# Two steps of the gated pairs' experts with each state in the first five parts of the recurrence, not only in the first

## The chip, the cores and the metric

The kernel runs on one core of one Trainium2 chip. The core has five engines that matter here: TensorE (PE for its matmuls, PEld for its weight loads), VectorE (DVE), ScalarE (ACT), GpSimd (POOL) and SyncE (SP, which only issues transfers in this kernel). Each engine works through its own queue of instructions in order, and they wait for each other by semaphores. The metric is the device time of one execution in microseconds (us), as the median of several runs.

## The reference

The program is a network of four layers on a batch of four sequences, 1024 rows of 128 features each, all in 32-bit floating point. Every layer has a mixing part and a feed-forward part, each followed by a residual and a layer norm. What matters here are the feed-forward part of the third layer and both parts of the fourth.

The third layer's feed-forward part picks two of eight experts for every row, and each expert is a gated pair of products ("gated pairs' experts" below):

```
h13 = einsum('bsh,ehi->bsei', x, w13);  gate, up = split(h13, 2)
h   = silu(gate) * up                              # 256 wide
y   = einsum('bsei,eih->bseh', h, w2)
out = sum over the two chosen experts of weight * y
```

The fourth layer's mixing part is a state-space recurrence, with 256 channels and 16 states per channel:

```
h   = exp(d_l[:, :, None] * A) * h + (d_l * x_l)[:, :, None] * b_l[:, None, :]
y_l = einsum('ben,bn->be', h, c_l)
```

The fourth layer's feed-forward part computes eight experts of width 512 for every row, without a choice in the products ("dense experts" below), and weighs them with a gate that keeps the most probable ones up to a sum of 0.8.

## The kernel before

The activations stay on the chip: `xN[b]` holds a batch's rows, `xT[b]` the same transposed. Layers one and two come first. Then the third layer's mixing part (`l2_attn`) runs over 128 units, and work of later parts is interleaved with it. The interleaving is done with Python generators: each part of the network is a generator that issues some instructions and yields, and a driver decides how often each one is advanced. The order in which instructions are issued in this way is their priority. A planner in the framework (`schedule_with_timeline_sim=True`) then sets the final order on each engine, taking by that priority what its own model of time finds ready. In `l2_attn` TensorE's order is taken from the program as it is; in the part that changes here the planner orders all engines. So the code's order is a strong guide to the queues, but not exactly the queues.

**The gated pairs' experts** are the generator `moe`, made by `l2_ffn`. For each batch, a router (`l2_dispatch`) ranks the experts of every row, and sixteen indirect transfers from POOL's queue (L1366, tile `xrows`) scatter the rows to a place in memory where rows of one expert are together. This gives 23 tiles of 128 rows per batch, 92 units for four batches. One step of the generator, at position `t`, does the following: every fourth step it loads four tiles of scattered rows for unit t+8 (SP); it loads the weights of unit t+4 (SP, L1441, tile `wx`, four buffers of 384 KB); it transposes rows for unit t+2 (every fourth step); it computes the hidden part of unit t (TensorE, then a tanh on ACT at L1473 and two products on DVE at L1474 and L1477); and it computes the output of unit t-2 (TensorE, a copy on ACT at L1493, and every fourth step a store from SP at L1495). A weight buffer is free for its next load once the output products have read it. When a batch's last tile is done, `l2_combine` starts and is advanced twice with each step: sixteen indirect gathers from POOL's queue (L1512, tile `yg`), a scaling on ACT, two additions on DVE (L1535, L1536) and a layer norm, after which the batch is marked "done". The generator yields without work while the scatters of the batch that it needs next are not all issued.

**The recurrence** works in halves: two for each of four batches, 512 positions each, eight in all (`l3`). `l3_prepare` computes a half's inputs. `l3_scan` runs its sixteen states. A state loads two rows `bn` and `cn`, broadcast to all partitions (SP, L1818, four buffers each); multiplies on POOL (L1823, tile `db`); computes a decay on ACT (L1827) and a scan on DVE (L1828) for each of two channel halves; and multiplies again on POOL (L1839, tile `hc`, four buffers). TensorE sums `hc` over the states in PSUM (tile `pys`); for batches 1 to 3 two states are first added by an accumulating transfer from POOL's queue (L1843). `l3_sum` and `l3_finish` end a half, with its output product, layer norm and router; the half then waits in the list `todo`.

**The dense experts** are the generator `work`, made by `l3_experts`. It takes halves from `todo` once they have aged by more than three states. A half's eight experts take six steps each: four with one hidden block (tile `ph`, ACT at L1951, tile `hh`) and two around the output products (tile `py`, added on DVE at L1967). Their weights are the tile `wh`, three buffers of 512 KB, loaded by SP (L1651).

**The driver** is the loop in `l3`. Before the scan of the second half of a batch it drains `moe` until the next batch is done. Then, with every state of the scan, it advances the end of the previous half, the preparation of the next half, the rest of the fourth batch's dispatch (which issues one scatter per state), `moe` once (and once more where i is 0), and `work` three times while `moe` still has steps and four times afterwards. All PSUM tiles of these parts but the scan's own share four banks (`ff`), and the experts, the preparation and the end of a half take them in turn.

Of the kernel before, what the change touches and what calls it, by code (L numbers as in the profile page):

```python
# [58 lines left out]
class Net:  # L59
# [1513 lines left out]
    def l3(self, moe, fp):  # L1573

        c3 = self.c3
        halves = [dict(b=b, h=h) for b in range(B) for h in range(2)]
        for i, u in enumerate(halves):  # L1580
            u["prev"] = halves[i - 1] if u["h"] else None
        halves[0] = dict(self.c3["first"], **{k: halves[0][k] for k in ("prev",)})
        for i, u in enumerate(halves[1:], 1):
            u["prev"] = halves[i - 1] if u["h"] else None
        work = self.l3_experts(fp)
        end = iter(())
        for i, u in enumerate(halves):
            nxt = iter(())
            if i + 1 < len(halves):
                if halves[i + 1]["h"] == 0:  # L1590
                    while "done" not in self.m2["st"][halves[i + 1]["b"]]:
                        next(moe)
                nxt = self.l3_prepare(halves[i + 1])
            for f in self.l3_scan(u):
                next(end, None)
                next(nxt, None)
                for k in range(1):
                    next(self.m2["rest"], None)
                busy = next(moe, moe) is not moe
                if i == 0:  # L1600
                    for k in range(1):
                        next(moe, None)
                for k in range(3 if busy else 4):
                    next(work)
                for v in c3["todo"]:
                    v["age"] += 1
            for f in chain(end, nxt):
                pass
            end = chain(self.l3_sum(u), self.l3_finish(u))
        for f in end:  # L1610
            next(work)
        c3["all"] = True
        for f in work:
            pass
# [563 lines left out]
```

## Time and profile before

| | |
|---|---|
| median of three runs | 2389.36 us (2387.49 to 2404.25) |
| the profiled execution | 2414.07 us, of which its span is 2412.3 us |
| granted TensorE clock, mean | 0.917 |
| busy PE, PEld | 2068.1 us (86%), 1454.9 us (60%) |
| busy DVE, ACT, POOL | 1420.2 us (59%), 1287.5 us (53%), 863.0 us (36%) |
| instructions | 34775 |
| transfers | 209.84 MB, mean 87 GB/s |

The profile is one execution on the chip. Times in its views are from the start of the span. A busy TensorE is not one at its peak, since its matmuls are pipelined and their ends are modelled. The profile's line for the granted clock gives tenths of full speed. Many instructions carry the line of a small helper (L127 for all matmuls, L131 for transposes), so they are told apart by the names of the tiles that they write and read. A matmul of 32-bit operands appears as two records. In a list of waits, the columns are the waiting engine and its tile and line, what ended the wait, the total in us, the number of waits and the longest.

### The profile page before, as it was taken

What the parts mean: (1) busy time and instruction counts of PE and PEld (TensorE: products, weight loads), DVE (VectorE), ACT (ScalarE), POOL (GpSimd) and SP (SyncE); (2) the same over time, 40 slices, a digit from 0 to 9 for tenths busy, and PEclk for the clock granted to TensorE, in tenths of its full rate; (3) what the DMA queues carried; (4) which work ended last, traced back from release to release, by engine and by line L of the source; (5) the groups of instructions that cost most, each with busy time, mean ns of one, the idle gap of its engine ahead of it and who ended that gap; (6) DMA issues with size and microseconds to landing.
All of it is one profiled execution on the core that took longest, in us unless ns stands there. A gap on an engine that the chain in (4) does not pass through costs nothing.

```text
span 2412.3 us, 34775 instructions
## 1 busy us (share of the span) xinstructions
PE 2068.1 (86%) x12170; PEld 1454.9 (60%) x12170; DVE 1420.2 (59%) x3949; ACT 1287.5 (53%) x2679; POOL 863.0 (36%) x557
## 2 busy tenths in 40 slices
PE   6767979979899999999979965778797989899888
PEld 3455655544577787787767753346564656565566
DVE  6457733433455655655555676777777777687421
ACT  6543433332455555555556555565757766767443
POOL 5001220000000011001020148888877879589400
PEclk9657989989999999999999987789998989999899
DMA  3000110022000010021222155456764657476411
GB/s 101 0 18 20 32 31 9 9 86 71 1 1 1 1 34 21 11 81 43 65 64 82 35 181 176 140 176 178 193 198 135 181 154 207 139 205 176 114 57 49
DMA packets 138512, 209.84 MB, mean 87 GB/s; under 512 B 18597, under 2 KB 75936, under 8 KB 138080
## 3 DMA queue, kind: packets, MB, share of 16 engines
q1 hardware_dynamic: 126048, 172.82, 23.2%
q0 software_dynamic: 12288, 34.79, 6.9%
q8 instruction: 96, 1.57, 0.3%
q14 instruction: 80, 0.66, 0.1%
HBM read 159.24 MB, written 23.16 MB: 76 GB/s over the span
## 4 chain that ended last, share of the span: by engine, by line
PE 60%; DVE 18%; ACT 10%; issue 7%; DMA 2%; POOL 1%; another core or an unknown queue 1%; SPq 0%; ACTq 0%; POOLq 0%; DVEq 0%
PE ph L127 12%; PE py L127 8%; PE po L1118 4%; PE pqk L127 4%; PE po L127 4%; PE pt L131 4%; PE pa_m L127 3%; DVE db L1828 3%; PE pys L127 3%; PE po L1134 3%; PE kp_mo L127 3%; PE pv L127 2%; PE pr L127 2%; DVE a L1105 1%; PE kp_mo L131 1%
## 5 line engine op out<-in xcount | busy, mean ns | idle before, releaser
L1839 POOL TENSOR_TENSOR hc<-db,cn 128x1024 f32<-128x1024 f32 x128 | 317.1, 2528 | 88.8 <-PE pys L127 41.8
L1823 POOL TENSOR_TENSOR db<-ud,bn 128x1024 f32<-128x1024 f32 x112 | 287.1, 2638 | 29.3 <-DVE pmv L159 23.2
L127 PEld LDWEIGHTS py<-wh,hh 128*128 128x128 f32 x2048 | 253.7, 197 | 70.5 <-issue 40.9
L127 PE MATMUL ph<-xT,wh 128*128 128x512 f32 x512 | 265.3, 637 | 33.5 <-DVE h_acc L1967 13.4
L127 PE MATMUL py<-wh,hh 128*128 128x128 f32 x2048 | 259.8, 281 | 14.6 <-ACT hh L1951 9.5
L1951 ACT ACTIVATE hh<-ph,sb_cols 128x512 f32<-128x512 f32 x256 | 171.8, 682 | 158.6 <-PE ph L127 127.2
L1151 DVE SCALAR_TENSOR_TENSOR num<-po,sb_c_trig,nsin 128x130 f32<-128x130 f32 x256 | 89.2, 348 | 268.5 <-ACT nsin L1150 251.2
L1827 ACT ACTIVATE da<-dl,aneg 128x512 f32<-128x512 f32 x224 | 153.3, 689 | 66.7 <-DVE db L1828 63.2
L127 PE MATMUL pys<-hc,sb_c_ident 128*128 128x512 f32 x320 | 168.6, 655 | 15.6 <-POOL hc L1839 8.2
L1026 POOL MEMSET cv<- 128x16 f32 x32 | 4.1, 128 | 482.6 <-ACT cv L1043 365.5
L1828 DVE TENSOR_TENSOR_SCAN db<-da,carry,db 128x512 f32<-128x512 f32 x128 | 157.4, 1268 | 20.4 <-POOL db L1823 10.2
L127 PEld LDWEIGHTS ph<-xT,wh 128*128 128x128 f32 x512 | 93.9, 204 | 123.6 <-issue 56.5
L1150 ACT ACTIVATE nsin<-po,sb_c_trig 128x130 f32<-128x130 f32 x256 | 94.8, 370 | 131.7 <-PE po L1134 72.3
L1828 DVE TENSOR_TENSOR_SCAN db<-da,db 128x512 f32<-128x512 f32 x128 | 149.6, 1206 | 14.3 <-ACT da L1827 6.7
L127 PE MATMUL pqk<-xT,wE 128*128 128x256 f32 x512 | 138.9, 395 | 16.7 <-DVE cv L1036 13.7
L1967 DVE SCALAR_TENSOR_TENSOR h_acc<-py,gt,h_acc 128x128 f32<-128x128 f32 x256 | 72.1, 343 | 130.3 <-PE py L127 125.0
L1366 POOL DMA_INDIRECT xrows<-xN,di x64 | 62.4, 976 | 238.1 <-ACT kN L1070 230.6
L1118 PE MATMUL po<-cv,a 128*128 128x130 f32 x1024 | 138.7, 279 | 1.0 <-DVE num L1151 0.8
L1118 PEld LDWEIGHTS po<-cv,a 128*128 128x128 f32 x1024 | 126.8, 194 | 5.1 <-PE pqk L127 1.1
L1043 ACT ACTIVATE cv<-cv,sb_c_trig 128x520 f32<-128x520 f32 x128 | 86.5, 724 | 77.3 <-DVE cv L1036 68.2
L127 PEld LDWEIGHTS pys<-hc,sb_c_ident 128*128 128x128 f32 x320 | 63.3, 211 | 85.3 <-issue 60.4
L127 PEld LDWEIGHTS pqk<-xT,wE 128*128 128x128 f32 x512 | 88.5, 192 | 36.3 <-DVE cv L1036 18.1
(456 smaller groups left out, 4492.9 us busy)
## 6 DMA issues: line engine op xcount, KB each, us to landing
wx<-in_wF SPq DMA_DIRECT2D x92, 384.0 KB
bn<-rows SPq DMA_DIRECT2D x128, 256.0 KB
cn<-rows SPq DMA_DIRECT2D x128, 256.0 KB
wh<-in_wH SPq DMA_DIRECT2D x64, 512.0 KB
hc<-hc POOLq DMA_DIRECT2D x48, 512.0 KB
xrows<-zero SPq DMA_DIRECT2D x4, 1472.0 KB
xg<-xrows SPq DMA_DIRECT2D x20, 256.0 KB
yrows<-ys SPq DMA_DIRECT2D x20, 256.0 KB
```

The costliest lines, as they stand in the source:

```text
L127: return self.nc.tensor.matmul(out=out, lhsT=lhsT, rhs=rhs, start=start, stop=stop)
L131: self.nc.tensor.transpose(out, in_, self.ident[0:n, 0:n])
L1043: nc.scalar.activation(Q["v"][c][:, hs, i, :], v1[:, hs, :], AF.Copy, scale=c2["trig"][:, k, i : i + 1],)
L1118: self.nc.tensor.matmul(out=u["po"][:, i, c, :], lhsT=u["a"][:, i, c, :], rhs=Q["v"][c][:, 2 * hp + i, :, :].rearrange("p a d -> p (a d)") ...
L1134: self.nc.tensor.matmul(out=u["po"][:, i, c, :], lhsT=u["q"][h, s], rhs=Q["st"][h, hp, c, :], start=False, stop=True, skip_group_check=True,)
L1150: nc.scalar.activation(t, po[:, :, c, VW : 2 * VW], AF.Copy, scale=trig[:, k, 1:2])
L1151: nc.vector.scalar_tensor_tensor(num[:, c], po[:, :, c, 0:VW], trig[:, k, 0:1], t, ALU.mult, ALU.add)
L1823: nc.gpsimd.tensor_mul(db, ud, bc[0])
L1827: nc.scalar.activation(da, dl[:, ec, :], AF.Exp, scale=aneg[:, j : j + 1])
L1828: nc.vector.tensor_tensor_scan(db[:, ec, :], da, db[:, ec, :], carry[:, ec, n : n + 1] if h else 0.0, ALU.mult, ALU.add,)
L1839: nc.gpsimd.tensor_mul(hc, db, bc[1])
L1951: nc.scalar.activation(ht, ph, AF.Relu, bias=self.col("h_b1", i=e * NK + k))
```

## The change

One condition in the driver's loop: the second step of the gated pairs' experts with each state is taken in halves 0 to 4 and no longer in half 0 alone.

```diff
                 busy = next(moe, moe) is not moe
-                if i == 0:
-                    for k in range(1):
-                        next(moe, None)
+
+                if i < 5:
+                    next(moe, None)
                 for k in range(3 if busy else 4):
                     next(work)
```

Here `i` counts the eight halves from 0. Where `moe` has no steps left, the added call returns at once and does nothing. What the steps issue is the same in both kernels, and so are the buffers and their numbers.

## The prediction

> **What bounds the kernel now.** I began with the page's forty slices. TensorE is dense except in slices 23 to 28 (one slice is 60.3 us), which is where GpSimd begins to work:
>
> ```profile
> PE   6767979979899999999979965778797989899888
> ...
> POOL 5001220000000011001020148888877879589400
> PEclk9657989989999999999999987789998989999899
> ```
>
> That stretch is the recurrence (`l3_scan`), eight halves of sixteen states. I cut it at the end of each half's last `hc` product (L1839) and asked for the busy time between the cuts; halves 0 to 7, columns PE, PEld, DVE, ACT, POOL, then granted clock, DMA share, GB/s:
>
> ```profile
> 1411.60:1551.90 140.30, 80.66 (x320) 51.63 (x320) 102.22 (x173) 72.37 (x162) 111.29 (x67) 0.77 0.55 176
> 1551.90:1654.50 102.60, 81.29 (x337) 52.89 (x338) 72.57 (x134) 63.16 (x128) 87.34 (x49) 0.84 0.53 157
> 1654.50:1763.20 108.70, 90.78 (x454) 61.65 (x453) 88.79 (x147) 70.34 (x147) 82.95 (x41) 0.94 0.70 198
> 1763.20:1881.90 118.70, 103.69 (x497) 67.68 (x496) 81.43 (x158) 79.71 (x147) 97.15 (x57) 0.93 0.58 164
> 1881.90:1978.70 96.80, 83.35 (x372) 50.71 (x371) 75.79 (x138) 69.18 (x129) 81.38 (x42) 0.93 0.64 172
> 1978.70:2058.20 79.50, 76.54 (x386) 50.81 (x386) 60.84 (x106) 51.23 (x86) 75.80 (x39) 1.00 0.67 182
> 2058.20:2171.10 112.90, 102.13 (x493) 65.71 (x491) 81.29 (x158) 81.10 (x139) 82.16 (x42) 0.95 0.65 180
> 2171.10:2258.20 87.10, 79.52 (x396) 52.65 (x396) 64.19 (x114) 56.09 (x87) 80.32 (x41) 0.96 0.64 173
> ```
>
> From half 1 on, a half lasts as long as its busiest engine plus 3 to 18 us: half 1 is POOL + 15.3, half 2 PE + 17.9, half 3 PE + 15.0, half 4 PE + 13.4. After half 7 about 154 us of experts remain on PE. The gated pairs' experts' share of PE, in halves 0 to 3 (tile `wx`, PE then PEld):
>
> ```profile
> 1411.60:1551.90 140.30, 36.05 (x216) 32.80 (x216) 0.77 0.55 176
> 1551.90:1654.50 102.60, 25.73 (x168) 24.10 (x168) 0.84 0.53 157
> 1654.50:1763.20 108.70, 19.05 (x132) 17.53 (x132) 0.94 0.70 198
> 1763.20:1881.90 118.70, 5.79 (x44) 5.62 (x44) 0.93 0.58 164
> ```
>
> A unit (one tile of 128 rows) has 12 records, so these halves run 18, 14, 11 and 3.7 units. Its other work, from the groups of halves 1 and 2 by shape (busy us, mean ns):
>
> ```profile
> L1477 DVE SCALAR_TENSOR_TENSOR mh<-sg,ph 128x256 f32<-128x256 f32 x25 | 10.3, 414 | 1.2
> L1474 DVE SCALAR_TENSOR_TENSOR sg<-sg,ph 128x256 f32<-128x256 f32 x25 | 10.3, 412 | 14.6 <-ACT sg L1473 14.5
> ...
> L1473 ACT ACTIVATE sg<-ph 128x256 f32<-128x256 f32 x25 | 9.4, 375 | 14.9 <-PE ph L127 8.6 <-remote 6.2
> ```
>
> In the lists of waits, half 2 and then half 3 show what happens when PE is loaded, and half 0 what two units per state met:
>
> ```profile
> POOL hc L1839 <- PE pys L127: 18.1, 2, 10.9
> ```
> ```profile
> POOL hc L1839 <- PE pys L127: 22.0, 3, 10.9
> ```
> ```profile
> PE ph L127 <- DMA wx<-in_wF: 7.5, 5, 3.2
> ```
>
> The recurrence's products stand still because the sums that free their buffers (`pys`) lie behind expert matmuls in PE's queue.
>
> **What moves, counted through the generators.** No instruction is added or removed. Half 0 keeps its two steps per state. In the code's order half 1 now takes units 61 to 91 (before: 61 to 76), so half 2 loses its fifteen; batch 2's combination ends at half 1, state 10 instead of half 2, state 5; batch 3's at half 2, state 10 instead of half 4, state 5. From then on the generator is empty, and the dense experts (`wh`) get four steps per state for three. This brings them forward by about 1.3 experts at the end of half 2, and no further: the second half's experts end at half 3, state 8 (before 13), then idle until the third half's router at state 13. From half 5 on the order is the old one, so halves 5 to 7 and the tail are costed at nothing. Nobody needs the early results: batch 2's are wanted before half 3 and batch 3's before half 5, and both were done in time.
>
> **Half 1.** +14 units in the cut: PE 14 x 1.84 (25.73/14) = 25.8, and a transpose each, 0.21 (5.4 us in 26 records), 2.9: 81.3 becomes 110.0. DVE +14 x 0.826 = 84.2. ACT +14 x (0.375 + 0.261 for the copy at L1493), and 3.5 copies of 0.58: 74.2. POOL stays 87.3; its sixteen gathers for batch 2 already lie here. The bound passes from POOL to PE. Lower end: the units use up all of PE's idle 21.3 us, 110.0 (+7). With the usual 13 on top: 123 (+20). Now the clock. The row gives 0.84 here and 0.94 in half 2, where a unit cost 19.05/11 = 1.73. [...] I take 3 us off: **+17**.
>
> [...] By the row: 157 GB/s x 102.6 us = 16.1 MB, plus 14 x 0.39 = 21.6 MB; over 120 us 180 GB/s, under the 198 that half 2 carried with 0.9 us of POOL's waits on such rows. [...] I go by the row, but not to zero: PE waited 7.5 us for weights over half 0's 18 units, which is 12.9 for 31; half 1 before showed no such wait on its list. Between 0 and 12.9 I take **+5**, since half 0 had a router and scatters in the way too.
>
> Behind these waits: on PE the `pys` sums, for which POOL waits; on SP, whose load at L1441 waits for one of four buffers (92.5 us in 34 waits from 1400 to 1900, the longest 8.9), the row loads, the dense experts' weights and the stores. Four `bn`/`cn` buffers cover four states, about 25 us; if that cover went, POOL would pay up to 8.9 each time.
>
> **Half 2.** PE 90.8 - 10 x (1.73 + 0.21) + 1.3 x 7.8 (500.4 us over 64 experts) = 81.5. POOL gets batch 3's sixteen gathers from half 3: 83.0 + 15.6 = 98.6, and with half 1's 15.3 idle (the other half with gathers) 114: **+5**.
>
> **Half 3.** PE 103.7 - 3.7 x 1.77 - 10.1 = 87, POOL 97.2 - 15.6 = 81.6: close to half 4 (83 and 81), so 87 + 13 = 100: **-19**; at least -10 (only the gathers and half their gaps), at most -25. **Half 4** loses nearly an expert, POOL binds at 81.4 + 13: **-2**.
>
> Sum: +17 + 5 + 5 - 19 - 2 = +6 us. The profiled execution took 2414.07 (span 2412.3 and 1.8 around it) and would take 2420; the median lies 1.0% below it and the sum is small, so 2389.4 + 6 = **2395**.
>
> **Rivals.** *The weight ring sets half 1's pace (slower).* A slot's cycle is load, gate matmuls, and two steps later the output matmuls that free it. The timeline's first matmuls of units 41 to 45 are 2.65 us apart with no recurrence running, those of units 52 to 60 are (1513.8 - 1451.9)/8 = 7.7 apart, at two per state. My half 1 (125 us) asks for 4.0 per unit. Nearly midway, at 5.0, it lasts 155: +52 + 5 - 19 - 2 = +36, 2425. It turns the verdict (over 24 us) from about 4.6. For it: half 0; against: half 0's holes are the fourth batch's router (11.3 us of PE on `sel`) and 16 scatters. *PE's holes take it all (faster).* Half 1 +7, less 6 for the clock, no weight wait; half 2 at 106 (-3) because `pys` is no longer late, half 3 -22, half 4 -2: -26, 2363. For it: 40 us of POOL waiting for `pys` in halves 2 and 3. *The change does nothing*, because the planner already places steps by readiness: 2389. Against: half 1's units came at the one-a-state pace, 6.4 us (76.8/12).
>
> **Chances.** Forecast 0.49, ring 0.33, holes 0.12, nothing 0.06. One per cent, 24 us, is about what a measurement of this kernel can tell from no change. Faster: 0.6 of the holes and a little of the forecast, 0.10. Slower: 0.85 of the ring and a tenth of the forecast, 0.33. The rest 0.57. Range: from the holes' edge, 2366, to a ring at 5.4 per unit (167 us, +48), 2437.
>
> **What would show it.** About 27 units' matmuls between the cuts of half 1 and hardly any in half 2; half 1 near 125 us with PE its busiest engine; batch 3's gathers in half 2; half 3 near 100; halves 5 to 7 and the tail alike within a few us. Half 1 above 140 with PE or SP standing before `wx` means the ring. I am wrong altogether if halves 5 to 7 move: then the planner has reordered more than the count tells.

## The result, and the profile after

The changed kernel is slower by 0.62%: the ratio of its time to that of the kernel before is 1.0062, with a 95% interval of 1.0048 to 1.0077. Its median is 2411.03 us over 12 runs (2405.79 to 2417.04), that of the kernel before 2396.49 us over 12 (2387.49 to 2405.74). The forecast was +0.25% and no change that can be told. The sum is near; what it is made of is not.

The page of the changed kernel, its profiled execution at 2405.79 us (span 2404.0, one slice 60.1 us):

```profile
PE   6767988979899999999989965878798889898988
...
POOL 5001310000000011011021167978786969688400
PEclk9657989989999999999999987879799989898999
```

POOL's later slices now swing between 6 and 9: it stops and starts again in the late halves. The same cuts as before, at the end of each half's last `hc` product, with the tail as a ninth row; columns PE, PEld, DVE, ACT, POOL (in the tail's row the entry after ACT is POOL's two records), granted clock, DMA share, GB/s:

```profile
1393.30:1530.30 137.00, 80.76 (x359) 56.06 (x359) 108.52 (x179) 73.99 (x168) 111.35 (x67) 0.80 0.61 189
1530.30:1638.30 108.00, 84.29 (x363) 54.74 (x364) 82.04 (x152) 67.59 (x142) 89.67 (x49) 0.82 0.58 174
1638.30:1765.70 127.40, 104.17 (x478) 67.19 (x477) 95.04 (x158) 84.10 (x169) 98.76 (x57) 0.87 0.58 158
1765.70:1850.70 85.00, 80.13 (x385) 51.13 (x385) 62.05 (x115) 55.24 (x96) 74.25 (x37) 1.00 0.70 179
1850.70:1950.20 99.50, 88.71 (x413) 55.85 (x412) 70.05 (x126) 69.66 (x128) 81.25 (x40) 0.95 0.61 163
1950.20:2054.90 104.70, 90.69 (x415) 56.65 (x414) 74.12 (x139) 69.93 (x115) 81.30 (x41) 0.90 0.61 170
2054.90:2156.70 101.80, 90.06 (x419) 56.69 (x418) 71.55 (x134) 66.02 (x116) 81.24 (x40) 0.93 0.67 180
2156.70:2255.20 98.50, 85.01 (x424) 56.21 (x423) 68.82 (x128) 62.15 (x94) 81.16 (x41) 0.93 0.63 164
2255.20:2404.00 148.80, 129.72 (x704) 90.75 (x704) 37.25 (x136) 58.33 (x94) 0.92 (x2) 0.95 0.20 56
```

Half 3 is 33.7 us shorter than before, half 2 is 18.7 longer, and halves 5 to 7, which the prediction left alone, last 305.0 us instead of 279.5. All of that lies in half 5, 104.7 us instead of 79.5; halves 6 and 7 last 200.3 us together, against 200.0. The gated pairs' experts came forward as intended (tile `wx`, PE then PEld, halves 0 to 3):

```profile
1393.30:1530.30 137.00, 40.88 (x252) 37.65 (x252) 0.80 0.61 189
1530.30:1638.30 108.00, 35.66 (x240) 32.91 (x240) 0.82 0.58 174
1638.30:1765.70 127.40, 8.63 (x68) 8.37 (x68) 0.87 0.58 158
1765.70:1850.70 85.00, 0.00 (x0) 0.00 (x0) 1.00 0.70 179
```

At 12 records a unit these are 21, 20, 5.7 and 0 units, against 18, 14, 11 and 3.7 before. The dense experts made room for them (tile `wh`, halves 1 and 2, after):

```profile
1530.30:1638.30 108.00, 0.00 (x0) 0.00 (x0) 0.82 0.58 174
1638.30:1765.70 127.40, 67.03 (x312) 44.50 (x313) 0.87 0.58 158
```

In the kernel before the same two halves held some of both:

```profile
1551.90:1654.50 102.60, 12.99 (x46) 7.96 (x47) 0.84 0.53 157
1654.50:1763.20 108.70, 45.91 (x227) 30.53 (x226) 0.94 0.70 198
```

So half 1's TensorE grew by only 3.0 us (in the second pair of profiles, below, it fell by 1.7), since 13.0 us of dense experts left it; they came back in half 2, which has 21.1 us more of them.

The later loss is in POOL's waits. From the end of half 3 to the end of half 7, the kernel before had these waits at the first product of a half (L1823, tile `db`; columns total, times, longest):

```profile
POOL db L1823 <- DVE pmv L159: 23.2, 1, 23.2
POOL db L1823 <- ACT dl L1788: 4.3, 1, 4.3
POOL db L1823 <- DVE gt L1910: 1.8, 1, 1.8
```

and the changed kernel these:

```profile
POOL db L1823 <- DVE ud L1787: 27.5, 2, 14.6
POOL db L1823 <- DVE pmv L159: 16.6, 1, 16.6
...
POOL db L1823 <- ACT dl L1788: 11.1, 1, 11.1
```

It waits at each of the four boundaries, 12.8, 16.6, 14.6 and 11.1 us, 55 in all against 29. The difference lies before halves 4 and 5, 29.4 us against 1.8; before halves 6 and 7 it is 25.7 against 27.5. A half's first product needs `dl` and `ud` from that half's preparation, so the recurrence stands still because the preparation is late. All waits below are named by the half that they come before.

Each kernel was run once more with a profile on one other chip, and cut in the same way. After minus before, in us:

| | forecast | first pair | second pair |
|---|---|---|---|
| half 0 | 0 | -3.3 | -0.1 |
| half 1 | +22 (17 and 5 for weights) | +5.4 | +5.4 |
| half 2 | +5 | +18.7 | +25.3 |
| half 3 | -19 | -33.7 | -33.7 |
| half 4 | -2 | +2.7 | +3.9 |
| halves 5 to 7 | 0 | +25.5 | +24.5 |
| tail | 0 | -5.3 | -5.1 |
| from the recurrence's start | +6 | +10.0 | +20.2 |

The two sums average 15.1 us; the timed medians differ by 14.5. What lies ahead of the recurrence is unchanged code, but took 1393 to 1417 us in these four profiles; so halves are compared from the recurrence's start. Chips differ too (the kernel before has medians of 2395 to 2422 us on them), so each ratio is against runs of the kernel before on the same chip.

### The profile page after: what moved, and what is told of

The parts are those of the page before. It is cut to its first block, busy times and chain, and to the rows that moved or that the text cites. A ratio compares the mean times of both kernels' runs of the same rounds, so it can differ in the third digit from the quotient of the medians.

```text
span 2404.0 us, 34783 instructions
## 1 busy us (share of the span) xinstructions
PE 2059.8 (86%) x12170; PEld 1446.3 (60%) x12170; DVE 1424.3 (59%) x3949; ACT 1293.2 (54%) x2684; POOL 862.7 (36%) x557
## 5 line engine op out<-in xcount | busy, mean ns | idle before, releaser
L1823 POOL TENSOR_TENSOR db<-ud,bn 128x1024 f32<-128x1024 f32 x112 | 283.0, 2575 | 55.2 <-DVE ud L1787 27.5
L127 PE MATMUL ph<-xT,wh 128*128 128x512 f32 x512 | 262.9, 632 | 22.5 <-DVE h_acc L1967 12.8
L127 PE MATMUL pys<-hc,sb_c_ident 128*128 128x512 f32 x320 | 173.0, 670 | 25.7 <-DMA hc<-hc 18.9
L127 PEld LDWEIGHTS pqk<-xT,wE 128*128 128x128 f32 x512 | 88.5, 192 | 31.0 <-DVE cv L1036 12.9
```

Of the source, the lines that this page charges most:

```text
L127: return self.nc.tensor.matmul(out=out, lhsT=lhsT, rhs=rhs, start=start, stop=stop)
L1823: nc.gpsimd.tensor_mul(db, ud, bc[0])
```

## The experiments

**The two kernels again**, for the table above.

> The kernel before, unchanged, for a second profile of it. In the first one the recurrence began at 1411.6 us, in the profile of the change at 1393.3, with the same instructions up to there; if that is noise of the first profile, it begins near 1395 here. The lengths of the eight halves (140, 103, 109, 119, 97, 80, 113, 87) should come back within about 5 us each if they are properties of the program; the theory that halves 4 to 7 are what the change lost needs their sum (376) to come back within about 8.

> The change, unchanged, for a second profile of it: halves near 137, 108, 127, 85, 100, 105, 102, 99, the sum of halves 4 to 7 near 404, and POOL idle for 11 to 17 us before the first product of each of halves 4 to 7.

2420.73 and 2436.66 us, one execution each. The kernel before came back to within 0.7 us in every half, the changed one within 1.2 except halves 0 and 2 (140.9 and 134.0). So a shift of 10 us in halves 5 to 7 is well above what repeats, one of 7 in half 2 is not.

**Which of the change's two consequences costs halves 5 to 7?** The loop couples two things: an extra step of `moe`, and, because `moe` then ends at half 2's state 10 instead of half 4's state 5, four steps of the dense experts per state for three over a stretch of 26 states. The two were taken apart. `three_steps` keeps the extra step and holds the dense experts to their old rate; `four_steps` is the kernel before with the new rate.

```diff
-                for k in range(3 if busy else 4):
+                for k in range(3 if busy or (i, s) < (4, 5) else 4):
```

```diff
-                for k in range(3 if busy else 4):
+                for k in range(3 if busy and (i, s) < (2, 11) else 4):
```

(`s` counts the states: `for s, f in enumerate(self.l3_scan(u))`.)

> The change, but the dense experts keep three steps per state up to half 4, state 4, as in the kernel before; only the gated pairs' experts come early. Theory 1 (the dense experts' fourth step uses up their backlog, half 3 ends early, and then the chain from the end of a half over its output product to the preparation of the half after next stands open at every boundary): the backlog stays, half 3 is 105 to 118, halves 4 to 7 sum to 376 to 388, and the time is 2395 to 2402, ratio 0.999 to 1.003. Theory 2 (the cost is the crowding of units into halves 1 and 2, where half 2 grew by 19 us): no difference from the change, 2408 to 2414, ratio 1.005 to 1.008.

> The kernel before with one step of the gated pairs' experts per state outside half 0, but four steps of the dense experts from half 2, state 11, as the change has it. Theory 1: this alone makes the loss, halves 4 to 7 sum to 395 to 405 and the time is 2404 to 2412, ratio 1.003 to 1.007. Theory 2: no loss, 2393 to 2400, ratio 0.998 to 1.002.

`four_steps`, with no extra step of `moe`, is as slow as the change: ratio 1.0066 (1.0040 to 1.0092). Its halves 4 to 7 last 404.8 us; the changed kernel's 404.6 and 405.1, those of the kernel before 376.3 and 376.5. Waits before halves 4 to 7: 8.0, 16.2, 14.1 and 11.4. `three_steps` has no wait at all before halves 4 and 5, and then, when its own fourth step has run for a while, 26.9 and 12.4 before halves 6 and 7; ratio 1.0025 (1.0013 to 1.0037). So the four steps alone are enough to make the loss, and where they begin later, the waits do too. But halves 4 to 7 of `three_steps` last 399.7 us, where 376 to 388 were expected. Only 10 us of the 23 over the kernel before are waits; these halves also hold 1366 records of the dense experts instead of 1298, nearly one expert more, since half 3 (87.8 us instead of 118.7) did fewer. So the extra step has a share of its own in the late halves: work that the early halves no longer do.

**Is the end of a half too slow in the code's order?** One theory was that the end and the preparation get one step per state each, and that a faster feed of the dense experts pushes them back; advancing both twice per state should then close the gaps.

```diff
-                next(end, None)
-                next(nxt, None)
+                for k in range(2):
+                    next(end, None)
+                    next(nxt, None)
```

The edit was put on the changed kernel (`after_pace`) and on the kernel before (`before_pace`).

> The change, with the end of the last half and the preparation of the next advanced twice per state instead of once, so that in the code's order a half's preparation is done by state 5 and not by state 9. Theory chain (what opens at the boundaries of halves 4 to 7 is the way from the end of half h-1 over its finish to the preparation of half h+1, paced by the states): POOL's idle time before halves 4 to 7 falls from 11 to 17 us each to under 5, halves 4 to 7 sum to 350 to 380 instead of 404, and the time falls under that of the kernel before, ratio 0.985 to 0.998. Theory queue (the chain is as long as its hops through loaded engines, whatever the code's order): idle time and sum stay, ratio 1.004 to 1.010.

> The same edit on the kernel before, which has this gap at two boundaries only (23 us before half 6, 4 before half 7). Theory chain: those two gaps close, halves 4 to 7 sum to 350 to 365 instead of 376, ratio 0.988 to 0.996. Theory queue: no gain, ratio 0.998 to 1.006.

It made both slower: 1.0130 (1.0105 to 1.0155) and 1.0070 (1.0043 to 1.0096). Gaps of 5 to 23 us stand before halves 3 to 7 of the first, 10 to 27 before halves 4 to 7 of the second. This theory fell. The skip product with which the end of a half begins (explained below) comes 79, 61 and 49 us after the ends of halves 3 to 5 in `after_pace`, where the changed kernel has 41, 44 and 42. By a count through the code a half's dense experts are then let in at state 8 of the next half and not at state 12, so they get eight states in front of the next skip product instead of four; the runs below show what that does.

**Does the supply set it?** A half brings eight experts of six steps, 48; its sixteen states take 48 at three steps each and 64 at four. At four, the dense experts use up what lies before them and pause until the next half is let in, some states after its router. Three steps throughout should leave no pause; it was put on both kernels.

```diff
-                for k in range(3 if busy else 4):
+                for k in range(3):
```

> The change, with the dense experts at three steps per state throughout, so that they take 48 steps per half for eight experts and never run ahead. Theory 1 (a backlog of dense experts is what hides the boundaries): POOL's idle time before halves 4 to 7 stays under 6 us each, halves 4 to 7 sum to 370 to 390, the tail is 150 to 165, ratio 0.997 to 1.003. Against it: the backlog hides nothing, boundaries stay open at 11 to 17 us and the tail grows on top, ratio 1.006 to 1.015.

> The kernel before, with the dense experts at three steps per state throughout. Theory 1: the gap of 23 us before half 6 closes and the tail grows by the experts left over, 0 to 20 us: ratio 0.994 to 1.003. Against it: the gap stays and the tail grows, ratio 1.003 to 1.010.

On the changed kernel the ratio to the kernel before is 0.9901 (0.9876 to 0.9925), 2397.35 us against 2418.24 on that chip: this version beats both kernels, and by more than the theory had. On the kernel before it is 0.9956 (0.9924 to 0.9987). The first's halves 4 to 7:

```profile
1884.00:1974.00 90.00, 83.93 (x405) 54.29 (x404) 70.79 (x128) 67.09 (x125) 81.18 (x42) 0.96 0.71 185
1974.00:2066.00 92.00, 84.67 (x389) 52.06 (x388) 71.40 (x127) 66.99 (x112) 81.22 (x41) 0.98 0.68 183
2066.00:2153.70 87.70, 82.53 (x407) 52.88 (x405) 70.47 (x134) 61.43 (x111) 81.13 (x40) 1.00 0.74 197
2153.70:2246.70 93.00, 88.75 (x447) 59.64 (x448) 66.18 (x122) 60.46 (x95) 81.12 (x40) 0.98 0.67 174
```

and its waits for a preparation in that stretch:

```profile
POOL db L1823 <- ACT dl L1788: 4.1, 1, 4.1
POOL db L1823 <- DVE ud L1787: 2.6, 1, 2.6
```

The four halves last 362.7 us instead of 404.6, POOL has the same 81 us in each, and 48 us of its waits are gone. Against `before_three`, the two steps are now a gain of 0.56% (2397.35 to 2410.80 us, four and five runs that do not overlap).

**What makes the preparation late.** A half's inputs go through two buffers (`xnT` and `xs`), so the preparation of half h+2 starts when half h's output product has read them, and that needs half h's skip product (`psk`, L1877). In the changed kernel, around the start of half 5, TensorE's timeline (start, duration, then idle time before in brackets) reads:

```profile
1951.10 3.73 PE L127 MATMUL py<-wh,hh 128*128 128x128 f32 x32
...
1967.37 1.01 PE L131 MATMUL pgt<-sb_c_ident,gt 128*8 128x128 f32 x4 [2.99 <-DVE pmv L159]
1972.35 2.07 PE L127 MATMUL pb<-sb_h_b,gT 8*128 8x128 f32 x8 [3.97 <-ACT gT L1925]
1974.35 6.33 PE L127 MATMUL ph<-xT,wh 128*128 128x512 f32 x8
...
1983.92 3.17 PE L127 MATMUL py<-wh,hh 128*128 128x128 f32 x26
...
1991.04 3.06 PE L127 MATMUL py<-wh,hh 128*128 128x128 f32 x26
1993.94 1.02 PE L127 MATMUL psk<-xnT,sb_s_in 128*128 128x512 f32 x2
```

The head of half 3's experts (`pgt`) stands in the queue before half 4's skip product and has to wait for half 3's router (`gt`, written at 1967.0, behind half 4's own sum in DVE's queue), and then for its own copy, 3.0 and 4.0 us. Between the two stand 64 records of `py`, two whole experts. Half 2's experts were used up at 1954.8, 19.5 us before half 3's first hidden block: that is the pause. Half 4 ended at 1950.2; its skip product runs 44 us later. In `after_three`, where half 4 ended at 1974.0:

```profile
1989.00 0.60 PE L131 MATMUL pgt<-sb_c_ident,gt 128*8 128x128 f32 x4
1989.44 3.29 PE L127 MATMUL py<-wh,hh 128*128 128x128 f32 x28
1992.66 1.15 PE L127 MATMUL pb<-sb_h_b,gT 8*128 8x128 f32 x8
...
2001.17 1.10 PE L127 MATMUL psk<-xnT,sb_s_in 128*128 128x512 f32 x2 [0.73 <-DVE ln_nm L168]
```

TensorE is still at the previous half's last expert (`py` right behind `pgt`), `pgt` and `pb` wait for nothing, and the skip product comes after 27 us. The same intervals for half 6, in us from the end of half 4:

| | tanh of the skip product | output product added | `dl` of half 6 ready | end of half 5 | POOL's wait |
|---|---|---|---|---|---|
| before | 32 | 45 | 107 | 79 | 23.2 |
| changed | 45 | 61 | 123 | 105 | 14.6 |
| `four_steps` | 44 | 60 | 121 | 104 | 14.1 |
| `after_three` | 31 | 46 | 98 | 92 | 2.6 |
| `before_three` | 22 | 38 | 94 | 101 | 0.0 |

From the tanh to `dl` it is 67 to 78 us in all of them. (The half's first product needs only the first of two parts of `dl`, and so starts some us before the time given.) With halves of 90 us, as an estimate from these figures, POOL waits unless the skip product is out within about 20 us. By that estimate the kernel before is no exception: it too takes four steps from half 4, state 5, on, its skip products come 31 and 47 us after halves 4 and 5, and it waits 23.2 us before half 6, since its half 5 took only 79.5.

What the change adds is that this begins earlier. The skip product of half 3, on which half 5 depends, runs in the kernel before (half 3 ended at 1881.9) and in the changed one (at 1850.7) at

```profile
1892.41 1.02 PE L127 MATMUL psk<-xnT,sb_s_in 128*128 128x512 f32 x2
```
```profile
1891.38 1.02 PE L127 MATMUL psk<-xnT,sb_s_in 128*128 128x512 f32 x2
```

so 11 and 41 us after the end of its half. A third pair of the buffers would cut the link itself; it was not tried.

**Which dense steps stand in the way?** By a count through the code a pause ends at a half's state 12, when the last half's experts are let in, and states 12 to 15 then issue sixteen steps, the head, the two experts seen above and two blocks of a third, ahead of the next half's first state and so of the skip product. The other candidate was the dense steps beside the end itself, in the next half's states 0 to 4. From half 3 on, `back_loaded` takes few steps there and more later, and still pauses (in states 9 to 11); `front_loaded` takes many there, fewer later, and does not run dry after half 3.

```diff
-                for k in range(3 if busy else 4):
+                for k in range(3 if busy else 4 if i < 3 else 2 if s < 5 else 5):
```

```diff
-                for k in range(3 if busy else 4):
+                for k in range(3 if busy else 4 if i < 3 else 5 if s < 5 else 2):
```

> The change, but from half 3 on the dense experts take two steps in each of the first five states of a half and five in each later one. In the code's order they still run dry in states 10 to 12, as in the change, but few of their matmuls stand ahead of the end of the last half. Theory ahead (experts queued ahead of the last half's skip product are what delays the way to the half after next): the tanh after the skip product comes 15 to 30 us after the end of its half instead of 42 to 45, POOL's idle time before halves 5 to 7 is under 6 us, halves 4 to 7 sum to 360 to 380, ratio 0.988 to 0.998. Theory dry (it is the pause while the experts wait for the next router that costs): nothing improves, sum 398 to 410, ratio 1.004 to 1.010.

> The reverse: from half 3 on five steps in each of the first five states and two later, 47 steps per half for the 48 that eight experts need, so that the experts never run dry after half 3 but crowd the first states. Theory ahead: the tanh comes 40 us or more after the end of its half, the gaps stay at 10 us or more, halves 4 to 7 sum to 395 to 415, ratio 1.003 to 1.012. Theory dry: the gaps close, sum 365 to 385, ratio 0.992 to 1.000 with a tail up to 10 us longer.

`back_loaded` has a ratio of 0.9994 (0.9982 to 1.0006), with waits of 0.0, 15.9, 5.0 and 5.0 and the tanh at 44, 45 and 41 us for halves 5 to 7, as late as in the changed kernel. `front_loaded`, with more steps beside the end, has 0.9941 (0.9920 to 0.9961), waits of 9.3, 0.0, 3.0 and 3.6, and the tanh at 25, 25 and 30. Halves 4 to 7 sum to 392.7 and 375.0 us: the first lies in the range of neither theory, the second in that of theory dry. The steps beside the end are not what delays the skip product. The early start of the new half's experts after a pause is left, and it fits that `back_loaded`, at five steps in states 12 to 15, puts three experts there; the next run tests it.

**Is it the pause, or what follows it?** `hold_start` keeps the four steps and makes the pause longer: from half 3 to half 6, the new half's experts are let in only at the first state of the next half, behind the skip product.

```diff
+            c3["hold"] = 7 if 3 <= i < 7 else 3
...
-            while len(heads) < 2 and c3["todo"] and ("all" in c3 or c3["todo"][0]["age"] > 3):
+            while len(heads) < 2 and c3["todo"] and ("all" in c3 or c3["todo"][0]["age"] > c3["hold"]):
```

> The change, but from half 3 to half 6 a half's dense experts are let in only at state 1 of the next half (aged by more than seven states instead of three), behind the first skip product of the half before, still at four steps per state. In the code's order they then pause in states 13 to 15 and 0, longer than in the change, but no step of theirs stands ahead of that skip product; in the change states 13 to 15 issue twelve steps, two experts, which wait on TensorE for the router at the boundary with the skip product behind them. Theory head of the queue (that is what opens the gaps): the tanh comes 12 to 30 us after the end of its half, POOL's idle time before halves 5 to 7 is under 6 us, halves 4 to 7 sum to 360 to 385, ratio 0.990 to 1.000. Theory dry (the pause itself costs, through TensorE's idle time and its lower clock): the gaps stay or grow, sum 400 to 420, ratio 1.005 to 1.015.

The skip product comes 2 us after half 4's end, before the head of half 3's experts (line numbers are one higher in the waits below, not here):

```profile
1971.92 1.02 PE L127 MATMUL psk<-xnT,sb_s_in 128*128 128x512 f32 x2
1972.78 0.60 PE L131 MATMUL pgt<-sb_c_ident,gt 128*8 128x128 f32 x4
```

and POOL's waits for a preparation between the ends of halves 3 and 7 are

```profile
POOL db L1824 <- DVE ud L1788: 12.9, 1, 12.9
POOL db L1824 <- issue: 3.3, 2, 1.9
```

The 12.9 is before half 4, whose skip product lies ahead of the edit's reach; before halves 5, 6 and 7 it is 0.0, 1.4 and 1.9 where the changed kernel has 16.6, 14.6 and 11.1. So the gap is made by what stands ahead of the skip product, not by the pause. But the ratio is 1.0049 (1.0034 to 1.0064): half 4 takes 115.0 us and the tail 154.3, and halves 4 to 7 come to 395.5, between what the two theories had. The experts that were held back have to be done later (702 records of them in the tail, 640 in the change). Closing the gaps in this way buys little; not pausing buys both.

**Does the number of halves matter?** With the extra step only in halves 0 and 1 (`if i < 2`), `moe` ends eleven states later by a count through the code, at half 3, state 5 (the expectation took it for three states at most).

```diff
-                if i < 5:
+                if i < 2:
```

> The change with i < 2 for i < 5: the second step in halves 0 and 1 only. In the code's order this moves only the last steps of the generator, by up to three states in half 2; the dense experts' fourth step begins at state 12 or 13 instead of 11. All theories: halves 4 to 7 sum to 398 to 408 and the ratio is 1.004 to 1.008. If it is far from that, the planner's answer to small shifts is as large as the effect itself, and the other runs must be read with that in mind.

0.9993 (0.9978 to 1.0007), which the expectation missed. The gaps are there (5.9, 22.9, 16.4 and 10.9), but half 4 lasts only 77.3 us before they set in fully, and halves 4 to 7 come to 390.6. From half 2 on, the first skip products later than 25 us are those of halves 3 and 4 (29 and 52 us), which fits the later start of the fourth step. But why the total then equals that of the kernel before, while `three_steps`, which starts it later still, is slower, stays open; differences of half a per cent between single variants here are to be read with that in mind. The step from the change to `after_three`, 1.6%, is well beyond them.

## Why the prediction was right and wrong

**The total was right, the account was not.** +6 us was forecast and some 15 came; both are below the 24 us named as tellable. But from half 0 to half 3 the forecast had +8 where the two pairs have -13 and -3, and from half 4 on it had -2 where they have +23. Two errors, of 11 to 21 us and of 25 us, cancelled for the most part, and that is luck. The prediction said that it is wrong altogether if halves 5 to 7 move. They moved by 25 us, and the planner's reordering is not needed to explain it: `four_steps`, which changes the dense experts' rate alone, moves them by 22.

**The step that failed** is "the second half's experts end at half 3, state 8 (before 13), then idle until the third half's router at state 13. From half 5 on the order is the old one, so halves 5 to 7 and the tail are costed at nothing". The idle states were counted, and priced at nothing, as idle time off the path. The count is nearly right (the next experts are let in at state 12), and the order of the dense experts from half 5 on is indeed the old one; halves 6 and 7 together did not move. The "so" is what fails, since a half's start is settled two halves before it. The runs show that a generator which has run dry changes what it issues next: it starts the new half's experts as soon as they are let in, and so in front of the skip product on which the preparation two halves later depends. At the end of half 3 the change issues fourteen steps of them there, the kernel before seven. Half 3's skip product comes 30 us later, half 5 waits 16.6 us instead of 1.8, and its TensorE is busy for 90.7 us instead of 76.5, at a granted clock of 0.90 instead of 1.00. The expense is 25 us, all in half 5; 5 come back in the tail.

**Half 1 (+22 forecast, +5.4).** Six units more lay in it, not fourteen: of the others, three came early, in half 0, and some five stayed in half 2. Its dense experts, 13.0 us of TensorE, moved out. The forecast added the units to the old 81.3 us as if nothing else could leave; TensorE measured 84.3, not 110. Its dense experts were there to be counted.

**The clock** was taken as 3 us of help in half 1, from 0.84 to the 0.94 of a busier half. No run shows these 3 us, nor the 6 us that the faster rival took off for it: the clock is 0.82 (in the second pair 0.87 before and 0.86 after), with TensorE busy for 78% of that half, where it was 79% before.

**The weight ring** was costed at +5 and was the rival on the slower side. Half 1 of the changed kernel has on its list of TensorE's waits

```profile
PE ph L127 <- DMA wx<-in_wF: 4.7, 4, 2.0
```

which is the size forecast, for six units more, and half 1's whole growth is 5.4. So the ring did not set the half's length on the chip, at 5.4 us per unit (108.0/20), although SP stood for 45.3 us before these loads (32.8 in the kernel before). The estimate from half 1's row, set against half 2's 198 GB/s with 0.9 us of POOL's waits on `cn` rows, held for what was moved: half 1 moved 174 GB/s, where 180 was estimated. In that half POOL waited for `bn` rows for 3.6 us (1.9 in the kernel before), and once for 7.0 us, put down to a load of `wx` (0.3 us of such waits before); its idle time as a whole went from 15.3 to 18.3 us. What made the planner place only six units more stays open; the ring in its own model of time was not tested.

**Half 2 (+5, measured +19 and +25).** The gathers for batch 3 are there as forecast (sixteen more on POOL, 98.8 us in all against an estimated 98.6). The mis-sized term is TensorE: 104.2 us, not 81.5, from the 21.1 us of dense experts where 10 (1.3 experts) were put, and from 5.7 units that stayed. (By the code the fourth step, from state 11 on, brings half 2 only five steps, 0.8 of an expert; most of the rest is the 13.0 us that left half 1.) On it POOL waits for `pys`, 17.2 us in 2 waits.

**Half 3 (-19, measured -33.7)** gained more than its lower end of -25: TensorE 80.1 us, not 87, POOL 74.3, not 81.6, at a granted clock of 1.00 (0.93 before), and 4.9 us above the busiest engine where 13 had been put. Half 4 was put at -2, for nearly an expert less, and lost 3: it has the first wait for a preparation, 12.8 us, and not less work but more, 323 records of dense experts instead of 285 and 88.7 us of TensorE instead of 83.4.

**The rivals.** The ring as the pace on the chip is excluded by TensorE's 4.7 us. TensorE's holes took what units came, and the early halves gain in sum, as this rival has it, but less (3 to 13 us, not 24) and not half by half: half 2 grew. What it did not have is the loss behind. Its support, "40 us of POOL waiting for `pys` in halves 2 and 3", is 29 us: the wait of 10.9 us stands before half 2's last product, which ends on the cut, and was counted in both lists. The change did something, so "nothing" falls by the table, though not by its total.

## What to carry to other kernels

When a change lets one stream of work end early, follow what shares its loop: count the supply and the demand of the next stream to the end of the kernel, and where it runs dry, look at what it issues first when it starts again and which product stands behind that in the same queue. Match the rate of a filler to its supply (here 48 steps per half over 16 states, three and not four), for a filler that is ahead of its supply stalls, and then bursts into the queue of the work that it was to fill around. A forecast that agrees in its sum is to be tested by its stages, since errors of 11 to 21 us and of 25 us cancelled here.

## What the runs showed of the hardware

TensorE's instructions took longer in its pause and just after it. Around the start of half 5 in the changed kernel, 53 us with 177 matmul records,

```profile
1950.00:2003.00 53.00, 40.48 (x177) 24.94 (x177) 34.82 (x67) 33.59 (x50) 35.26 (x18) 0.81 0.57 170
```

and in `after_three` at the same place, 41 us with 184,

```profile
1974.00:2015.00 41.00, 39.08 (x184) 24.31 (x183) 29.26 (x49) 29.41 (x47) 40.85 (x22) 1.00 0.74 203
```

the granted clock is 0.81 in the first and 1.00 in the second, and more records take less busy time. It was low in one piece, which outlasts the pause (its last wait ends at 1972.4):

```profile
1959.20:1979.70 20.50, 12.15 (x23) 5.58 (x24) 11.48 (x20) 11.77 (x19) 11.66 (x6) 0.50 0.31 93
```

In the first TensorE had waits of 4.8 us in two for `hc` (the longest 4.0), 4.0 for `gT` and 3.0 for the router. It is seen in single instructions too: the four transposes `pgt` took 1.01 us after the pause and 0.60 without it, the eight matmuls `pb` 2.07 and 1.15. Whether the pauses or the amount of work made the clock low is not shown: no run here separates the two. In half 1, with more gated pairs' experts and fewer dense ones, TensorE was busy for 78% of the time at a clock of 0.82, and in the kernel before for 79% at 0.84.
